# Graph network kernel: the later edge passes take 36 instead of 40 node tiles as products with counts

## The chip, the cores and the metric

The kernel runs on one core of one Trainium2 chip. The metric is the device time of one execution in microseconds (us); lower is better. The engines are named as in the profile: PE multiplies matrices, PEld loads its weights, DVE and ACT work on vectors, POOL issues the indirect DMAs (gathers and scatters by row indices), and SP issues most of the plain DMAs.

## The reference, cut to what matters

A graph of 12500 nodes with 128 features and 200000 edges passes through four layers, each followed by a residual and a layer norm. Each layer adds up, for every node, rows of the nodes at the other end of its edges. Three of the four sums are plain (no weight on the edge once the rows are scaled):

```
msgs = feats[edge_src] * norm[:, None]
agg  = segment_sum(msgs, edge_dst, num_segments=n)        # layer 1, then a top-2 mixture of 64 experts
h    = segment_sum(xs[s], d, num_segments=N)              # layer 2
agg  = segment_sum(x[src], dst, num_segments=x.shape[0])  # layer 3
```

The edges are sorted by `dst`, and `dst` is drawn as `12500 * u ** 2` with `u` uniform. So low node numbers have many edges and high ones few: about half of the edges end in the first quarter of the nodes. `src` is uniform.

## The kernel before, in words

Nodes are handled in 98 tiles of 128, edges in 391 steps of 512 (four chunks of 128). Rows of features are kept in HBM tables as three bfloat16 parts whose sum is the float32 value, so a matrix product with a table tile is three products.

The stages follow one another:

1. `spread_edges` and `collect_edges` (up to about 2860 us of the profile) do the weighted first layer and bring, for every tile of source nodes, its edges' destinations into `hs` and `hd`.
2. The first plain pass, `edge_sums(AT, tables[0], later=0)` (about 2866 to 3915 us).
3. Routing (to about 4240 us), the 64 experts (about 4246 to 4825 us) and the combining of their outputs (about 4830 to 5120 us), then the batch norm (to about 5300 us).
4. The second plain pass, `edge_sums(AT, tables[1])`, about 5304 to 6042 us, and its node work.
5. The third plain pass, `edge_sums(AT, tables[2])`, about 6220 to 6955 us, and its node work to the end.

A plain pass (`fast_sums`, L1059) adds up the edges in two ways at once. Destinations below `HT[later] * 128` are taken as **products with counts**: for each tile of source nodes there is a matrix of counts (128 sources x destinations, how many edges lead from one to the other), and `dense += x^T counts` (L1089), in banks of 512 destinations, three products per bank. Destinations above are **gathered**: from edge step `LS[later]` on, every chunk of 128 edges has its source rows fetched by an indirect DMA on POOL (`fg<-table,e_row`, L1098), and multiplied by a 128 x 96 matrix of 0 and 1 made by DVE (`fh`, L1104) into a window of 512 destinations (`fps`, L1115). A window is `WC = 16` chunks, that is four steps; it begins with a product with zeros (L1166), and DVE adds it to the sums `AT` at its end (L1175). Edges that a gathered step has below the limit are masked in `e_loc`.

Band 0 is node tiles 0 to 24 (six banks). Its counts are built in the first pass (`Counter`) and written to HBM (`counts[0]`). Band 1 is node tiles 24 to 40 (four banks). Its counts are built while the experts run (48 of the 98 source tiles, L1367) and while their outputs are combined (the other 50, L1398), by `band_counts` (L1183): DVE makes the marks `fs` (L1037) and `fd` (L1039, as wide as the window of destinations that a twelfth of the tile's edges can reach), PE multiplies them (`fb_ps`, L1053), ACT casts each bank (L1055), SP writes the tile's counts to HBM (L1057). The second and third pass load both bands' counts (`fc_a<-counts`) and the source tile (`fc_x<-table`), three buffers each.

Inside a pass the order on PE, DVE, ACT and POOL is the program's (`manual_schedule`, L1148). The work of the products is a list of steps (one bank of one source tile each); it is dealt out evenly over the windows but the last:

```
per = -(-total // (nw - 1))
...
mine = min(per, left)
...
upto = WC * (m + 1) // max(1, mine)
```

In a window, after each step of products, PE does as many chunks as are due. POOL's list holds only the gathers, issued a window ahead, into twelve buffers of four chunks (`fgat`), which is three windows. With `HT = (24, 40)` and `LS = (191, 247)` a later pass has 98 x 10 + 2 = 982 steps and (391 - 247) / 4 = 36 windows, so 29 steps to a window.

In the expert and combining stages the order on each engine comes from a scheduler. An expert is seven transposes (L1348) whose result DVE copies (L1349, L1350), products with the first weights (L1355), the activation on ACT (L1357), fourteen products with the second weights (L1362), and an addition on DVE (L1365). In combining, each of 98 tiles takes two gathers on POOL (`yk<-ybuf,come`, L1402, twelve buffers), which DVE adds (L1405).

Of the kernel before, what the change touches and what calls it, by code (L numbers as in the profile page):

```python
# [55 lines left out]
MID = NB // 2  # L56
SG = 2 * GM
W3 = 3 * W0 + 6
HT = (24, 40)

HB = 12
LS = (191, 247)
LB = EB // P * LS[0]
NLB = NBLK - LB
LW = 96
# [53 lines left out]

BANDS = Band(0, HT[0]), Band(HT[0], HT[1])  # L120
WM = max(max(b.cols) for b in BANDS)
# [4 lines left out]
def gnn_kernel(ctx: ExitStack, tc: tile.TileContext, a, out: bass.AP):  # L126
# [43 lines left out]
    e_loc = [const.tile([P, NLB], BF16, name=f"e_loc{i}") for i in range(2)]  # L170
    l_slot = const.tile([1, NB - LS[0]], I32, name="l_slot")
    l_base = const.tile([1, (NB - LS[0]) // 4], I32, name="l_base")
    iota_h = const.tile([P, WM], FP16, name="iota_h")
# [159 lines left out]
    def window_slots(pool, first, bad):  # L333

        n = NB - LS[0]
        f = pool.tile([1, n // 4, 4], F32, name="ws_f")
        V.tensor_copy(f.rearrange("o w q -> o (w q)"), first[:, LS[0]:NB])
        V.tensor_copy(l_base, f[:, :, 0])
        for i in range(2):
            V.tensor_scalar(bad[0:1, 10 + i:11 + i], f[:, (LS[i] - LS[0]) // 4, 0:1], float(HT[i] * P), None, op0=OP.is_ge)  # L340
        d = pool.tile([1, n // 4, 4], F32, name="ws_d")
# [111 lines left out]
    def spread_edges(bad):  # L453
# [5 lines left out]
        with tc.tile_pool(name="sc", bufs=1) as pc, tc.tile_pool(name="scp", bufs=1, space=PSUM) as pps:  # L459
# [30 lines left out]
            if True:  # L490
# [3 lines left out]
                with tc.tile_pool(name="rf", bufs=1) as pa, tc.tile_pool(name="rfp", bufs=2, space=PSUM) as tp_:  # L494
# [56 lines left out]
                    for i in range(2):  # L551

                        m = pa.tile([P, NLB], F32, name="in_band")
                        V.tensor_scalar(m, to_c, float(HT[i] * P), -1.0e3, op0=OP.is_lt, op1=OP.mult)
                        V.tensor_tensor(e_loc[i], place, m, OP.add)
# [503 lines left out]
    def fast_sums(AT, table, later):  # L1059
# [7 lines left out]
        with ExitStack() as st:  # L1067
# [5 lines left out]
            V.memset(zeros_b, 0.0)  # L1073
            V.memset(AT[:, HT[later] * P - BANK:], 0.0)
            if build:
# [443 lines left out]
```

## Time and profile before

| | |
|---|---|
| median of 10 runs | 7157.5 us (7154.34 to 7164.61) |
| profiled execution | 7158.06 us, span 7156.3 us |
| PE busy | 5137.7 us (72%) |
| DVE busy | 4252.7 us (59%) |
| POOL busy | 3861.0 us (54%) |
| ACT busy | 2000.4 us (28%) |
| gathers L1098 | 1952, 988 ns each |
| products L1089 | 7424 recorded, 381 ns each |
| moved by DMA | 1375.92 MB, 192 GB/s over the span |

The durations of products are from start to modelled end and overlap; what a product costs in a row of products is read from the distance of their starts. The busy shares are of the whole span, over stages with different limits. Gathers of the three passes share one line: 800 of the 1952 are in the first pass, 576 in each later one.

### The profile page before, as it was taken

What the parts mean: (1) busy time and instruction counts of PE and PEld (TensorE: products, weight loads), DVE (VectorE), ACT (ScalarE), POOL (GpSimd) and SP (SyncE); (2) the same over time, 40 slices, a digit from 0 to 9 for tenths busy, and PEclk for the clock granted to TensorE, in tenths of its full rate; (3) what the DMA queues carried; (4) which work ended last, traced back from release to release, by engine and by line L of the source; (5) the groups of instructions that cost most, each with busy time, mean ns of one, the idle gap of its engine ahead of it and who ended that gap; (6) DMA issues with size and microseconds to landing.
All of it is one profiled execution on the core that took longest, in us unless ns stands there. A gap on an engine that the chain in (4) does not pass through costs nothing. (4 is left out here: it accounts for less than half of the span.)

```text
span 7156.3 us, 106164 instructions
## 1 busy us (share of the span) xinstructions
PE 5137.7 (72%) x32622; PEld 3146.0 (44%) x33009; DVE 4252.7 (59%) x11539; ACT 2000.4 (28%) x4124; POOL 3861.0 (54%) x3917
## 2 busy tenths in 40 slices
PE   0666666666665664899996659998539998299995
PEld 0444444444442332455553437663215554155544
DVE  6887777777785777767673854549861112611115
ACT  3333333333331222333331114444420000300003
POOL 0677777777771000777777550007427775177760
PEclk7555555555557887999997669999769998599998
DMA  9976545555558997455553125554358886588862
GB/s 249 268 222 202 156 152 152 152 151 152 152 148 271 322 321 229 153 166 167 165 164 119 39 90 166 165 159 134 127 176 294 287 282 216 165 292 290 282 227 67
DMA packets 1045604, 1375.92 MB, mean 192 GB/s; under 512 B 106204, under 2 KB 848216, under 8 KB 1045038
## 3 DMA queue, kind: packets, MB, share of 16 engines
q1 hardware_dynamic: 802680, 960.66, 43.9%
q0 software_dynamic: 181312, 376.38, 16.8%
q10 hardware_dynamic: 61046, 31.77, 1.6%
q8 instruction: 301, 4.93, 0.3%
q14 instruction: 265, 2.17, 0.1%
HBM read 911.40 MB, written 457.00 MB: 191 GB/s over the span
## 5 line engine op out<-in xcount | busy, mean ns | idle before, releaser
L1098 POOL DMA_INDIRECT fg<-table,e_row x1952 | 1928.5, 988 | 1658.5 <-SPq L987 681.4
L1089 PE MATMUL dense<-fc_a,fc_x 128*128 128x512 bf16 x7424 | 1870.1, 381 | 253.1 <-DMA fc_x<-table 185.8
L715 POOL DMA_INDIRECT msg<-rows,to x1564 | 1509.3, 965 | 656.9 <-issue 381.1
L1089 PEld LDWEIGHTS <-fc_x 128*128 128x128 bf16 x7644 | 678.4, 98 | 830.9 <-issue 249.9
L1175 DVE TENSOR_TENSOR AT<-AT,fps 128x512 f32 x122 | 84.0, 688 | 1606.8 <-PE fps L1115 1583.7
L1053 PE MATMUL fb_ps<-fd,fs 128*128 128x512 bf16 (+7 forms) x3942 | 879.2, 341 | 88.5 <-DMA fg<-table,e_row 44.3
L665 PE MATMUL g_ps<-rows,minus 128*128 128x258 bf16 x1564 | 462.8, 400 | 617.7 <-ACT rows L698 583.4
L698 ACT CAST rows<-g_ps 128x516 bf16<-128x516 f32 x1173 | 698.7, 596 | 647.1 <-PE g_ps L665 294.8
L659 PE MATMUL g_ps<-win,hot 128*128 128x129 bf16 x4692 | 651.0, 311 | 238.5 <-DMA win<-table 120.1
L1039 DVE TENSOR_SCALAR fd<-iota_h,hd 128x128 bf16<-128x128 f16 (+6 forms) x1563 | 786.7, 509 | 0.0
L1115 PEld LDWEIGHTS <-fg 128*128 128x128 bf16 x5856 | 463.4, 98 | 517.5 <-DMA fg<-table,e_row 86.1
L659 PEld LDWEIGHTS <-hot 128*128 128x128 bf16 x4692 | 534.4, 143 | 318.9 <-issue 199.5
L1115 PE MATMUL fps<-fh,fg 128*128 128x96 bf16 x5856 | 579.4, 209 | 86.9 <-DMA fg<-table,e_row 68.7
L831 PE MATMUL ce_sum<-ce_r,ce_s 128*128 128x390 bf16 x1764 | 380.9, 383 | 274.9 <-DVE ce_s L828 269.0
L1402 POOL DMA_INDIRECT yk<-ybuf,come x196 | 219.8, 1121 | 652.6 <-DMA counts<-bc_a 593.1
L1053 PEld LDWEIGHTS <-fs 128*128 128x128 bf16 x4108 | 377.7, 98 | 387.6 <-issue 124.4
L665 PEld LDWEIGHTS <-minus 128*128 128x128 bf16 x1564 | 199.8, 128 | 744.3 <-issue 743.9
L1055 ACT CAST fc_a<-fb_ps 128x512 bf16<-128x512 f32 x588 | 344.1, 585 | 633.0 <-PE fb_ps L1053 615.4
L643 DVE TENSOR_TENSOR_SCAN run_ps<-one_ps,run_ps,bin 99x512 f32<-99x512 f32 x390 | 505.4, 1296 | 13.8
L1037 DVE TENSOR_SCALAR fs<-iota_b,hs 128x128 bf16<-128x128 bf16 x1563 | 409.5, 264 | 38.3 <-PE fb_ps L1053 34.7
L831 PEld LDWEIGHTS <-ce_s 128*128 128x128 bf16 x1764 | 190.3, 112 | 465.5 <-DVE ce_s L828 261.3
L232 ACT ACTIVATE ln_sq<-zz,ln_m 128x128 f32<-128x128 f32 x392 | 152.0, 389 | 813.2 <-DVE ln_m L228 813.2
(378 smaller groups left out, 6299.6 us busy)
## 6 DMA issues: line engine op xcount, KB each, us to landing
ce_r<-msg SPq DMA_DIRECT2D x98, 1782.0 KB
fc_a<-counts SPq DMA_DIRECT2D x196, 768.0 KB
fc_a<-counts SPq DMA_DIRECT2D x196, 512.0 KB
rb<-rows_d SPq DMA_DIRECT2D x391, 256.0 KB
counts<-fc_a SPq DMA_DIRECT2D x98, 768.0 KB
counts<-bc_a SPq DMA_DIRECT2D x98, 512.0 KB
fc_x<-table SPq DMA_DIRECT2D x490, 96.0 KB
msg<-blank SPq DMA_DIRECT2D x99, 396.0 KB
```

Of the source, the lines that this page charges most:

```text
L643: V.tensor_tensor_scan(c, one_ps, b, st["end"], OP.mult, OP.add)
L659: T.matmul(gps[i][:, q, 0:D + 1], hot[i][:, q * P:(q + 1) * P], win[i][:, k, :], start=(q == 2 * half and k == 0), stop=False)
L665: T.matmul(gps[i][:, 2 * h:2 * h + 2, 0:D + 1], minus, r[:, 2 * h:2 * h + 2, k * W0:k * W0 + D + 1], start=False, stop=True, skip_group_ch ...
L698: S.copy(r[:, :, k * W0:k * W0 + D + 1], gt)
L715: sc = G.indirect_dma_start(out=msg[:, :], out_offset=bass.IndirectOffsetOnAxis(ap=to[:, q:q + 1], axis=0), in_=r[:, q, :], in_offset=None)
L831: T.matmul(ps, sel[:, j, :], r[:, j, 0:3 * W0], start=(j == 0), stop=(j == RB - 1))
L1037: V.tensor_scalar(sel, iota_b, hs[:, s, j:j + 1], None, op0=OP.is_equal)
L1039: V.tensor_scalar(col[:, 0:hi - lo], iota_h[:, 0:hi - lo], hd[self.i][:, s, q:q + 1], None, op0=OP.is_equal)
L1053: T.matmul(ps[:, lo - c0:hi - c0], self.sel[s, j], self.col[s, j][:, lo - w[j][0]:hi - w[j][0]], start=(j == first), stop=(j == js[-1]))
L1089: T.matmul(dense[n], xr[s][:, k, :], cnt[s][:, n * BANK:(n + 1) * BANK], start=(s == 0 and k == 0), stop=(s == NT - 1 and k == 2))
L1098: G.indirect_dma_start(out=g[q][:, i].rearrange("p k f -> p (k f)"), out_offset=None, in_=table[:, :], in_offset=bass.IndirectOffsetOnAxis ...
L1115: T.matmul(ps[:, ds(at[0], LW)], g[i // 4][:, i % 4, k, :], hot[i // 4][:, i % 4, :], start=False, stop=(i == WC - 1 and k == 2))
```

## The change

Two constants change; no function does.

```diff
-HT = (24, 40)
+HT = (24, 36)
 
 HB = 12
-LS = (191, 247)
+LS = (191, 235)
```

Band 1 becomes node tiles 24 to 36, three banks instead of four. The later passes have 98 x 9 + 2 = 884 steps of products, and gather the edges from step 235 on, twelve steps more: (391 - 235) / 4 = 39 windows, 624 gathers a pass, and 24 steps to a window. `band_counts` makes three banks per source tile: of an ordinary tile the 17 products with marks become 13 (the four of the last bank, 512 columns each, fall away), and the six marks `fd` that were 2048, 2048, 1472, 1216, 640 and 320 wide become 1536, 1536, 1216, 960, 320 and 128 wide. A tile's counts in HBM shrink from 512 to 384 KB. The first pass keeps its band 0 and its step 191.

## The prediction

> **What bounds the kernel now.** I began with the page: its busy rows show where the engines are full. The page's slices (tenths of busy time, each 178.9 us):
>
> ```profile
> PE   0666666666665664899996659998539998299995
> POOL 0677777777771000777777550007427775177760
> PEclk7555555555557887999997669999769998599998
> ```
>
> Four stretches have PE at 9: the first edge pass (slices 17 to 20, counted from 0), the experts (24 to 26) and the two later edge passes (30 to 32 and 35 to 38). POOL stands at 7 in all three passes. "9" and "7" suggest that PE is the bound and POOL has a quarter to spare. So I asked for busy time, granted clock and DMA in stretches inside these stages; the columns are length, then PE, PEld, DVE, ACT, POOL busy us (instructions), clock, DMA share, GB/s.
>
> ```profile
> 3850.00:3910.00 60.00, 24.09 (x147) 14.79 (x147) 7.68 (x15) 0.00 (x0) 45.52 (x48) 0.50 0.28 78
> 4250.00:4820.00 570.00, 566.10 (x3395) 399.41 (x3456) 291.42 (x703) 245.06 (x430) 0.00 (x0) 1.00 0.56 164
> 4850.00:5100.00 250.00, 209.61 (x822) 83.88 (x838) 230.69 (x726) 114.65 (x199) 196.95 (x175) 0.99 0.41 139
> 5400.00:6000.00 600.00, 594.49 (x3791) 302.82 (x3866) 76.48 (x149) 0.00 (x0) 455.25 (x476) 1.00 0.86 286
> 6300.00:6900.00 600.00, 595.74 (x3798) 303.11 (x3873) 74.39 (x144) 0.00 (x0) 455.33 (x476) 1.00 0.86 287
> ```
>
> Row 1 is the end of the first pass, where the products are done and only gathers are left: PE idles, the DMA engines are at 0.28, and POOL still shows 76% busy. Thus 76% is a POOL that is full. POOL's waits in the second pass say why (who waited for whom: total us, times, longest):
>
> ```profile
> POOL fg L1098 <- issue: 137.1, 439, 3.6
> POOL fg L1098 <- PE dense L1089: 19.5, 64, 0.3
> POOL fg L1098 <- PE fps L1115: 11.9, 39, 0.3
> ```
>
> Every gather has the same 0.30 us of idle time before it, whoever is named; once 3.6, at the start. POOL never waits for a buffer that PE must free. POOL's timeline gives its pace; one row each early and late in the second pass, then in the third (start, us):
>
> ```profile
> 5319.90 0.94 POOL L1098 DMA_INDIRECT fg<-table,e_row  x1 [3.62 <-issue]
> ...
> 6037.21 0.95 POOL L1098 DMA_INDIRECT fg<-table,e_row  x1 [0.30 <-issue]
> 6227.41 0.95 POOL L1098 DMA_INDIRECT fg<-table,e_row  x1 [0.30 <-issue]
> ...
> 6950.51 0.94 POOL L1098 DMA_INDIRECT fg<-table,e_row  x1 [0.30 <-issue]
> ```
>
> The first is gather 8 of 576 and the second the last: 717.3 us / 568 = 1.263 us. The third is gather 4: 723.1 / 572 = 1.264 us. In the stretch of row 1 it is 1.26 us as well, so neither DMA load nor PE makes this pace. A window of 16 gathers costs POOL 20.2 us. PE needs 21.0 us for it now (zeroing products at 5990.52 and 6011.56 us); it falls behind by up to two windows, which the three windows of buffers hold, and catches up in the last two windows, which have no products. Both engines thus end the pass within a microsecond or so of each other: PE is full, and POOL is full too.
>
> **The change, part by part.** *Later passes.* Removed per pass: 98 source tiles x 1 bank x 3 = 294 products of 512 columns. Six take 1.30 us in PE's rows, so one takes 0.2165 us: -63.7 us of PE work. Added: three windows (39 for 36), 144 products of 96 columns at 0.043 us (three in 0.13 us between products) and three zeroings at 0.22: +6.8 us on PE. Added on POOL: 48 gathers x 1.263 = +60.6 us, and none removed. The steps of a window fall from 29 to 24 (884 of them over 38), so PE needs 24 x 0.65 + 16 x 0.13 + 0.22 = 17.9 us against POOL's 20.2. The products' saving becomes waiting, and the pass follows POOL: +60.6 us, twice, is +121.3. The order of instructions shows that POOL's list grows by exactly 48 in each pass. What follows the last gather stays: its landing (6950.51 to 6954.19 us in the third pass), three small products and one addition.
>
> At nothing: the wider clearing of AT on DVE (512 more of 8448 columns in 7.1 us, 0.4 us) and 12 more comparisons and three more additions for the gathers run on a DVE that is 13% busy; uncovered they would cost 0.4 + 12 x 0.55 + 3 x 0.69 = 9 us a pass. The loads fall from 512 to 384 KB per source tile and pass, in a queue that is at 0.86 and will have more time.
>
> *Experts.* 48 source tiles of counts are built here, now with 13 instead of 17 products on PE, which is 99% busy. The four that go have 512 columns: 192 x 0.2165 = -41.6 us by their own length. The rows offer a second reading. Their lines below are the last group of products of experts four apart, early and late (start, us):
>
> ```profile
> 4285.63 3.27 PE L1362 MATMUL pw<-w,hT 128*112 128x128 f32 x28
> 4318.56 3.27 PE L1362 MATMUL pw<-w,hT 128*112 128x128 f32 x28
> ...
> 4441.21 3.28 PE L1362 MATMUL pw<-w,hT 128*112 128x128 f32 x28
> 4478.24 3.27 PE L1362 MATMUL pw<-w,hT 128*112 128x128 f32 x28
> ```
>
> Early, four experts take 32.93 us with 34 count products between them (two tiles); late, 37.03 with 51 (three). A tile is 7744 columns, 3.27 us at 0.2165 per 512, yet the third costs 4.10: late in the stage the marks of L1037 and L1039 stand on DVE ahead of the copies of L1349 that the next expert waits for. In the order of the changed kernel nearly all experts have the early form (26 count products to three experts, the copies right behind L1365). Early form: (32.93 - 2 x 3.27) / 4 = 6.60 us per expert without counts. New stage: 64 x 6.60 + 558 products (42.9 tiles of 5696 columns, 2.41 us) = 526, against 578 now (4246.3 to 4824.5): -52 us. I take -48, nearer to the second, since it is read from rows of the very pattern; range -40 to -54. Lost cover: the early form keeps 6 or 7 count products between L1348 and L1355, 1.2 us for a copy of about 1.0.
>
> *Combining.* 50 tiles are counted while POOL gathers yk back to back (4830.06 to 5108.28 us, 1.427 us each; the last bracket shows again only 0.3 us waits):
>
> ```profile
> L1402 POOL DMA_INDIRECT yk<-ybuf,come x196 | 219.8, 1121 | 652.6 <-DMA counts<-bc_a 593.1 <-DVE fs L1037 20.1 <-DMA yk<-ybuf,come 17.1
> ```
>
> Here a gather lasts 1121 ns, against 946 for the median fg: 34 us over, while DVE is 92% busy. The marks shrink: widths 2048, 2048, 1472, 1216, 640, 320 took 745, 745, 593, 541, 376, 308 ns; at 1536, 1536, 1216, 960, 320, 128 I interpolate 610, 610, 541, 465, 308, 250, so 0.53 us less per tile, 26 us in all. If POOL's pace ignored that, the gain were 0; if DVE set the stage, 26. The rows say POOL sets it and is stretched beside DVE; the marks, 75 us of L1037 and 164 of L1039, lose 26 of 240: by share 34 x 26 / 240 = 4 us, more if long marks delay more. I take -6, and -2 for the eight products that the last two tiles lose behind the last gather. [...]
>
> **Sum:** +121.3 - 48 - 8 = +65. The profiled execution took 7158.06 us (span 7156.3), 0.6 above the median of the ten: 7158 + 65 = 7223 us.
>
> **Rivals.** *A: PE is the bound, so the kernel gets faster.* For it: PE at 99%, and the chain of waits puts 82% of the second pass on the products. Then each pass changes by -63.7 + 6.8 = -57, and the sum is -114 - 56 = -170: 6988 us. It would need a gather pace of (727 - 57) / 624 = 1.07 us or less. The whole change breaks even when a pass grows by 28 us, that is at (576 x 1.263 + 28) / 624 = 1.21 us; no start-to-start distance of fg rows in the stretches that I read is under 1.24. Chance 4%.
>
> *B: the clock.* PE will wait in the later passes, and waits cost it clock. In the first pass's end:
>
> ```profile
> 3842.39 0.43 PE L1115 MATMUL fps<-fh,fg 128*128 128x96 bf16 x3 [2.42 <-DMA fg<-table,e_row]
> ...
> 3843.64 1.48 PE L1089 MATMUL dense<-fc_a,fc_x 128*128 128x512 bf16 x3
> ```
>
> After a wait of 2.42 us three products take 1.48 us instead of 0.81, for some 4 us. PE needs 17.9 of 20.2 us, so it becomes the bound where the mean clock falls below 0.89; at 0.75 a window is 23.9 us, 37 of them 884 against 794 for the whole pass, +90 twice: about 7400 us. Against it: the combining stretch is 84% busy with many waits at a clock of 0.99, a chunk's wait here is about 2.3 / 16 = 0.14 us, and a PE that falls behind no longer waits. Chance 6%. [...]
>
> *C: something like nothing.* POOL's pace eased to about 1.21, or gains outside the passes doubled: 7158 us, 2%. That the change doesn't do what it says needs edges below step 235 beyond node 4607, and the branch to the general path; the reference's inputs have node 4522 there, so under 1%.
>
> **How the numbers follow.** My forecast has 88%. Low end: passes +118 (added gathers at 1.23), experts -54, combining -26: +38, 7196. High end: passes +123 (at 1.28), experts -40, combining 0, and up to 9 for half-clock stretches behind waits: +92, 7250. The rivals lie outside, so the range holds about 85%. A measurement of this kernel tells 0.2% (14 us) from no change. Faster has A's 4%, same C's 2%, slower the rest, 94%.
>
> **What would show it.** Right: 624 gathers per pass at 1.26 us from end to end, still only 0.3 us before each; PE in the passes below 90% with waits for fg; passes about 60 us longer; experts about 48 shorter. Wrong: gathers that wait, a pace under 1.21, a clock under 0.89 in the passes, or an expert period that stays at 9 us.

## The result and the profile after

The changed kernel took 7206.76 us (median of 8 runs, 7204.25 to 7210.37), the kernel before 7157.5 us on the same chip (28 runs, 7148.0 to 7164.61). The ratio is 1.007, 95% interval 1.0061 to 1.0079: 49 us slower. The forecast was 65 us slower, 7223. The profiled execution of the changed kernel took 7201.54 us, span 7199.8. Four later runs, those with halved marks, were timed while the kernel before itself took 8278 to 8426 us, so of their times only the ratio to it is read.

The page's slices of the changed kernel, each now 180 us:

```profile
PE   0666666666665653999996659987089994499975
POOL 0677777777771000777776640037077773477760
PEclk7555555555557887999997679999599996799988
```

PE still stands at 8 and 9 in the two later passes (slices 29 to 32 and 35 to 37), POOL at 7. By this view alone little has happened. The stretches show more. The first row lies in the experts, the second in the combining, the third and fourth in the later passes; the columns are length, then PE, PEld, DVE, ACT, POOL busy us (instructions), granted clock, DMA share, GB/s.

```profile
4250.00:4770.00 520.00, 514.57 (x3193) 381.48 (x3253) 262.33 (x682) 208.50 (x379) 0.00 (x0) 1.00 0.56 166
4790.00:5040.00 250.00, 187.86 (x701) 76.28 (x712) 224.68 (x785) 95.69 (x166) 192.15 (x190) 0.95 0.38 126
5250.00:5900.00 650.00, 604.73 (x3810) 306.66 (x3885) 84.25 (x163) 0.00 (x0) 493.41 (x515) 1.00 0.82 261
6250.00:6900.00 650.00, 601.10 (x3799) 305.38 (x3874) 84.05 (x163) 0.00 (x0) 493.74 (x514) 1.00 0.81 261
```

In the passes PE went from 99% to 604.73 / 650 = 93% at a clock of 1.00, and POOL is at 493.41 / 650 = 76%, the share of a POOL that is full. Who waits for whom in the second pass of the changed kernel (total us, times, longest): first POOL's longest groups of waits, then PE's.

```profile
POOL fg L1098 <- issue: 157.3, 505, 3.6
POOL fg L1098 <- PE dense L1089: 19.5, 64, 0.3
POOL fg L1098 <- DMA fg<-table,e_row: 8.5, 28, 0.3
```

```profile
PE fps L1115 <- DMA fg<-table,e_row: 63.4, 75, 3.7
PE fps L1115 <- issue: 5.7, 18, 0.5
```

POOL still never waits for a buffer: 0.3 us before every gather, and once 3.6 at the start, as before. PE now waits for gathers that have not landed, 63.4 us in one pass, where the kernel before has 3.0 us. POOL's timeline gives the pace: gather 9 of the second pass and its last one, number 623, counted from 0.

```profile
5247.38 0.94 POOL L1098 DMA_INDIRECT fg<-table,e_row  x1 [0.30 <-issue]
...
6022.99 0.95 POOL L1098 DMA_INDIRECT fg<-table,e_row  x1 [0.30 <-issue]
```

775.6 us / 614 = 1.263 us, as before. The stages side by side, in us, each from the first or last start of the instructions named:

| stage | before | after | difference | forecast |
|---|---|---|---|---|
| to the experts (first L1348) | 4246.3 | 4244.5 | -1.8 | 0 |
| experts (first L1348 to last L1362) | 578.1 | 531.6 | -46.5 | -48 |
| to the first yk | 5.7 | 5.9 | +0.2 | 0 |
| combining: first to last yk | 278.2 | 256.8 | -21.4 | -6 |
| last yk to the second pass's first gather | 195.4 | 189.8 | -5.6 | -2 |
| second pass, first to last gather | 733.5 | 794.4 | +60.9 | +60.6 |
| to the third pass | 183.2 | 182.2 | -1.0 | 0 |
| third pass, first to last gather | 730.1 | 792.6 | +62.5 | +60.6 |
| to the end | 205.8 | 202.1 | -3.7 | 0 |

The differences add to +43.6, the two spans differ by 43.5. Two of the three big terms, the passes and the experts, hold to about 2 us. The third, combining, is three times what I forecast:

```profile
L1402 POOL DMA_INDIRECT yk<-ybuf,come x196 | 198.3, 1012 | 605.7 <-DMA counts<-bc_a 546.3
```

A gather of yk takes 1012 ns on average where it took 1121, and 196 x 0.109 = 21.4 us is the whole of that stage's gain.

### The profile page after: what moved, and what is told of

It is laid out like the page before. It is cut to its first block, busy times and chain, and to the rows that moved or that the text cites. A ratio compares the mean times of both kernels' runs of the same rounds, so it can differ in the third digit from the quotient of the medians.

```text
span 7199.8 us, 105218 instructions
## 1 busy us (share of the span) xinstructions
PE 5012.6 (70%) x31949; PEld 3093.2 (43%) x32324; DVE 4215.2 (59%) x11567; ACT 1936.2 (27%) x4026; POOL 3931.7 (55%) x4013
## 5 line engine op out<-in xcount | busy, mean ns | idle before, releaser
L1098 POOL DMA_INDIRECT fg<-table,e_row x2048 | 2023.7, 988 | 1677.3 <-SPq L987 678.0
L1089 PE MATMUL dense<-fc_a,fc_x 128*128 128x512 bf16 x6842 | 1770.0, 381 | 254.4 <-DMA fc_x<-table 244.9
L1089 PEld LDWEIGHTS <-fc_x 128*128 128x128 bf16 x7056 | 611.8, 98 | 751.6 <-DMA fc_x<-table 194.6
L1053 PE MATMUL fb_ps<-fd,fs 128*128 128x512 bf16 (+6 forms) x3557 | 775.5, 338 | 92.8 <-DMA fg<-table,e_row 44.3
L1115 PE MATMUL fps<-fh,fg 128*128 128x96 bf16 x6144 | 659.7, 208 | 233.1 <-DMA fg<-table,e_row 190.6
L1115 PEld LDWEIGHTS <-fg 128*128 128x128 bf16 x6144 | 500.3, 98 | 734.5 <-DMA fg<-table,e_row 286.6
L1039 DVE TENSOR_SCALAR fd<-iota_h,hd 128x128 bf16<-128x128 f16 (+5 forms) x1563 | 733.9, 475 | 0.0
L1402 POOL DMA_INDIRECT yk<-ybuf,come x196 | 198.3, 1012 | 605.7 <-DMA counts<-bc_a 546.3
L1053 PEld LDWEIGHTS <-fs 128*128 128x128 bf16 x3717 | 342.7, 98 | 357.7 <-issue 114.7
```

The source lines that it names most:

```text
L1039: V.tensor_scalar(col[:, 0:hi - lo], iota_h[:, 0:hi - lo], hd[self.i][:, s, q:q + 1], None, op0=OP.is_equal)
L1053: T.matmul(ps[:, lo - c0:hi - c0], self.sel[s, j], self.col[s, j][:, lo - w[j][0]:hi - w[j][0]], start=(j == first), stop=(j == js[-1]))
L1089: T.matmul(dense[n], xr[s][:, k, :], cnt[s][:, n * BANK:(n + 1) * BANK], start=(s == 0 and k == 0), stop=(s == NT - 1 and k == 2))
L1098: G.indirect_dma_start(out=g[q][:, i].rearrange("p k f -> p (k f)"), out_offset=None, in_=table[:, :], in_offset=bass.IndirectOffsetOnAxis ...
L1115: T.matmul(ps[:, ds(at[0], LW)], g[i // 4][:, i % 4, k, :], hot[i // 4][:, i % 4, :], start=False, stop=(i == WC - 1 and k == 2))
```

## The experiments

My theory: POOL's pace of 1.26 us per gather sets the later passes; PE's saving there is worth nothing; the gains lie in the experts, where PE is full, and in the combining, where the marks on DVE lengthen POOL's gathers. The rival of the first part is that PE is the bound of the passes (A). The rivals of the last part are that the fourth bank's products, casts and writes made the difference, or the busy DVE as such.

**The gathers alone.** Against the kernel before: forty tiles stay as products with counts, twelve more steps are gathered.

```diff
-LS = (191, 247)
+LS = (191, 235)
...
-            V.memset(AT[:, HT[later] * P - BANK:], 0.0)
+            V.memset(AT[:, HT[later] * P - (1 + later) * BANK:], 0.0)
```

> Half of the change alone: the later passes gather from step 235 on (39 windows, 624 gathers) but keep the products of 40 node tiles, and band 1 keeps four banks of counts; edges below node 5120 are masked in the added windows, so the sums stay whole. AT is cleared from 512 columns earlier. Theory (POOL's pace of 1.26 us sets the later passes): 48 gathers x 1.263 = +61 us per pass, first to last gather 794 us as in the changed kernel; PE needs 26 x 0.65 + 2.3 = 19.2 us of the 20.2 us window and still waits; experts and combining as before; 7157 + 122 = 7279 us (7270 to 7290). Rival (PE sets them): only +6.8 us per pass for the small products, 7171 us, and POOL with idle times over 0.3 us.

Measured: 7287.17 us, ratio 1.0175 (1.0158 to 1.0192), 125 us slower. The passes' gathers take 798.6 and 794.2 us, at 1.27 us each; experts (578.8) and combining (280.4) are as before.

**The products alone.** The kernel before, in whose later passes the last bank of band 1 is left out. No gather is added.

```diff
+        use = (BANDS[0].banks, BANDS[1].banks - 1)
...
-                        for n in range(BANDS[b].banks):
+                        for n in range(use[b]):
```

> The other half alone: the kernel before, whose later passes leave out the products of the last bank of band 1 (294 products a pass) and add no gather; counts are built and loaded in full. The sums of node tiles 36 to 40 are left out. Theory (POOL's pace): 576 gathers still take 727 us, so each pass changes by -3 to +1 us, although PE loses 64 us of work; PE busy in the passes falls to about 92%; 7150 to 7158 us. Rival (PE sets them): -64 us per pass, 7030 us.

Measured: 7167.92 us, ratio 1.0009 (0.9999 to 1.0018). That is 10 us above the top of the range expected, and no run isolates why. Taking 64 us of work from PE in each pass bought nothing: 736.4 and 733.6 us from first to last gather, some 3 us more than before. The stretch of the second pass, first of the gathers-only kernel, then of this one:

```profile
5350.00:5950.00 600.00, 577.71 (x3663) 294.01 (x3736) 77.53 (x151) 0.00 (x0) 456.09 (x473) 1.00 0.83 272
```

```profile
5350.00:5950.00 600.00, 563.39 (x3635) 284.01 (x3707) 76.33 (x148) 0.00 (x0) 455.79 (x474) 1.00 0.89 292
```

PE's share differs from kernel to kernel, POOL's is 456 of 600 in both and 455 before; the passes follow the number of gathers and not PE's work. Rival A is dead: it had 7171 for the gathers alone and 7030 here.

**The changed kernel without its added gathers**: 36 windows.

```diff
-        nw = (NB - LS[later]) // (WC // 4)
+        nw = (NB - LS[later]) // (WC // 4) - 3 * later
```

> The changed kernel without its added gathers: the later passes take three windows fewer than they need (36 windows from step 235 on); the edges of the last twelve steps are left out. It holds the experts, the combining and the fewer products of the change. Theory: the passes are as long as before (734 us first to last gather), experts -47 and combining -27 us as in the changed kernel, 7157 - 77 = 7080 us (7072 to 7088), which is 125 us below the changed kernel for 96 gathers, 1.26 to 1.30 us each. Rival (PE sets the passes): a further -64 us per pass, 6955 us.

Measured: 7093.39 us, ratio 0.9909 (0.9892 to 0.9925): 68 us below the kernel before on the same chip (7161.59), and 5 us above the range expected; the profiled execution, 7085.78, lies inside it. The passes' gathers take 736.9 and 733.0 us, as with the products alone; the experts take 531.5 us, yk's stretch 260.3. This is what experts and combining give by themselves, and the changed kernel spends it, and 49 us more, on its added gathers.

**Old widths of the marks.** The changed kernel, but in the combining stage each mark `fd` is made as wide as before; the added columns are not used.

```diff
+                wide = self.i == 1 and s >= EXB
+                mk = {1536: 2048, 1216: 1472, 960: 1216, 320: 640, 128: 320}.get(hi - lo, hi - lo) if wide else hi - lo
...
-                V.tensor_scalar(col[:, 0:hi - lo], iota_h[:, 0:hi - lo], hd[self.i][:, s, q:q + 1], None,
+                V.tensor_scalar(col[:, 0:mk], iota_h[:, 0:mk], hd[self.i][:, s, q:q + 1], None,
```

> The changed kernel, with the marks fd of the combining stage drawn as wide as before (2048, 2048, 1472, 1216, 640, 320; the columns beyond the three banks are not used). Products, casts and writes stay as in the changed kernel. Theory (POOL's gathers yk are stretched beside DVE's marks, and narrower marks are why combining lost 27 us where 8 were forecast): the yk gathers return from 1012 to about 1110 ns, combining to within 5 us of before, 7207 + 22 = 7229 us (7222 to 7234). Rival (the stretch came from the products, casts or writes of the fourth bank): yk stays near 1012 ns, 7207 us. Proportional rule (delay by the share of marks' time): 4 us, 7211 us.

Measured: 7232.15 us, ratio 1.0098 (1.0081 to 1.0115), where the changed kernel has 1.007. The yk row of the run without added gathers, then of this one, both from one chip:

```profile
L1402 POOL DMA_INDIRECT yk<-ybuf,come x196 | 202.0, 1030 | 605.9 <-DMA counts<-bc_a 546.5
```

```profile
L1404 POOL DMA_INDIRECT yk<-ybuf,come x196 | 214.8, 1096 | 606.4 <-DMA counts<-bc_a 546.9
```

The width alone puts back 66 ns a gather, to 1096 ns where about 1110 was expected; yk's stretch is 272.8 us. Over the profiles with four banks, all their marks and 50 tiles in the combining (278.2, 280.4 and 276.5) the mean is 278.4; over those with three and narrow marks (256.8, 260.3 and 257.1, the last from the run that comes next) it is 258.1. So 14.7 of the 20.3 us are the widths (12.5 by the two runs of one chip); for the other 5.6 no run here isolates a cause.

**The fourth bank without its marks.** The changed kernel, in whose combining stage each tile repeats one bank's products and cast and writes 128 KB more.

```diff
+        if s >= EXB:
+            u = cp.tile([P, BANK], BF16, name="bc_u")
+            maker.bank(s, 2, u, again=True)
+            Y.dma_start(spare[s], u)
```

> The changed kernel; in the combining stage each tile repeats one bank's products and its cast, and writes 128 KB more to a spare tensor: the fourth bank's work on PE, ACT and DMA without the wider marks. Theory (marks alone make the difference): yk at 1012 to 1040 ns, its stretch 257 to 263 us, the kernel 7205 to 7214. Rival (the bank's products, cast and write matter): yk back at about 1100 ns, stretch 272 to 278 us, the kernel 7221 to 7229.

Measured: 7216.46 us, ratio 1.0081 (1.0066 to 1.0097), 2.5 us above the theory's range and 4.5 below the rival's; yk 1013 ns, its stretch 257.1 us. The bank's products, casts and writes leave the gathers as they were (1012 ns without them). They lengthen what follows the last gather by 2.3 us (192.1 against 189.8).

**No marks.** The kernel before; tiles up to 96 of the combining stage reuse the marks of two earlier tiles, so their counts are not their own, while products, casts and writes stay in the program.

```diff
-        maker.marks(s, 0, 1)
+        if EXB + 2 <= s < NT - 1:
+            for j in BANDS[1].used(s):
+                for d in (maker.sel, maker.col):
+                    d[s, j] = d[EXB + s % 2, j]
+            dummy(s)
+        else:
+            maker.marks(s, 0, 1)
```

> The kernel before, with 36 windows and four banks of counts. Left out: in the combining stage no marks are made for the tiles up to 96; the products, casts and writes of their counts stay and use the marks of two earlier tiles, so these counts are wrong. Theory (marks on DVE lengthen POOL's gathers): yk falls from 1121 ns to about 950 ns, the pace to about 1.25 us, the stretch of yk from 278 to about 245 us, the kernel by 34 to 40 us, to about 7121. Rival (products, casts or count writes lengthen the gathers, or POOL's pace is what it is): yk stays at 1100 to 1120 ns, the kernel within 7 us of before, about 7157.

Here `dummy` does nothing. Measured: 7234.04 us, ratio 1.0107 (1.0091 to 1.0122), which neither theory expected. The stage itself did as the theory says, yk 961 ns and a stretch of 246.8 us:

```profile
L1411 POOL DMA_INDIRECT yk<-ybuf,come x196 | 188.3, 961 | 652.1 <-DMA counts<-bc_a 592.7
```

But from the last yk to the second pass it is 298.9 us instead of 195.4. ACT's timeline (start, us) has the reason:

```profile
4964.03 0.58 ACT L1055 CAST bc_a<-fb_ps 128x512 bf16<-128x512 f32 x1 [0.55 <-PE fb_ps L1053]
5076.91 1.28 ACT L210 ACT_TABLE_LOAD   x1 [112.29 <-DVE d L1435]
```

Without the marks the scheduler's order differs: an operation of the batch norm stands on ACT's list ahead of the remaining casts. It waits 112 us for DVE, which is adding up yk; the casts queue behind it, PE's products behind the casts, and 103 us of counting are left over after the last gather. The total of this run says nothing of the marks; its gathers do. But from 4964 us on they ran beside hardly any products, casts or writes, so the gathers before that count: the first 14, still beside marks, average 1124 ns, the 94 that start between 4846 and 4964 us, beside products, casts and writes and without marks, 951.

**Reductions in the place of marks.** As above, but `dummy` keeps DVE busy.

```diff
+        for w in (570, 570, 430, 370, 220, 150):
+            for n in (100, w):
+                d = dkp[0].tile([P, 1], F32, name="dm")
+                V.tensor_reduce(d, iota_h[:, 0:n], AX.X, OP.add)
```

> As the run without marks, but in their place DVE does twelve reductions a tile of about the same time in all (one input from SBUF, one column out; 570, 570, 430, 370, 220 and 150 elements and six of 100), so that DVE is as busy as before. The counts are wrong in the same way. Theory (it is the form of the marks that holds up POOL's gathers): yk stays near 950 ns, the kernel at 7115 to 7130. Rival (any busy DVE lengthens them): yk near 1110 ns, the kernel at about 7155.

Measured: 7138.42 us, ratio 0.9969 (0.9958 to 0.998), 8 us above the range of the theory; here products, casts and writes go on through the whole stage. The yk row, the stretch of the combining, and DVE's timeline there:

```profile
L1417 POOL DMA_INDIRECT yk<-ybuf,come x196 | 192.2, 981 | 652.8 <-DMA counts<-bc_a 593.4
```

```profile
4845.00:5085.00 240.00, 211.29 (x890) 96.27 (x908) 235.40 (x760) 124.85 (x216) 182.90 (x188) 0.93 0.48 159
```

```profile
4900.04 3.83 DVE L1190 TENSOR_REDUCE dm<-iota_h 128x1 f32<-128x100 f16 x12
4903.79 0.86 DVE L1420 SCALAR_TENSOR_TENSOR ACC<-yk,gates,ACC 128x128 f32<-128x128 f32 x3
```

The twelve reductions of a tile take 3.75 us from start to start; the twelve marks of a tile in the kernel before take 3.78 (4902.72 to 4906.50 us in its timeline). DVE is even busier than before, 235.40 of 240 us, and the gathers are 140 ns shorter; the stretch is 250.7 us. So what lengthened the gathers was not that DVE is busy (981 ns beside reductions, 961 beside neither reductions nor marks, 1121 beside the marks), and DVE was not the bound of the stage. It is these marks that do it.

**Fewer tiles beside the experts.** The kernel before with `EXB = 44` instead of 48.

> The kernel before with 44 instead of 48 tiles counted beside the experts, so 54 instead of 50 in the combining stage. If a tile of counts costs the experts 4.1 us (the late row) they fall by 16, at 3.27 by 13. In the combining stage the tiles' marks stretch at most: stretch of yk in proportion to the excess per tile, 34 x 4 / 50 = +3, up to +10 if the added tiles also wait. Sum -3 to -13: 7145 to 7155. Rival (the combining stage is full and takes a tile at DVE's price of 5.3 us): +21 - 16 = +5, 7163.

Measured: 7153.81 us, ratio 0.9992 (0.9983 to 1.0001), inside the forecast and not told apart from no change. The experts lose 15.9 us (562.2), 4.0 for each tile: the price that the late rows of the prediction showed. The combining takes 9.7 back, and after the last yk 3.8 us fall away. It is the best version with all the work that ran here, and no more than a hint.

**Halved marks.** By my rows of single gathers, long marks delay out of proportion. In the timeline of before, a gather that starts ahead of two marks of 2048 columns reads:

```profile
4908.49 1.47 POOL L1402 DMA_INDIRECT yk<-ybuf,come  x1 [0.30 <-DVE fd L1039]
```

```profile
4909.03 0.74 DVE L1039 TENSOR_SCALAR fd<-iota_h,hd 128x2048 bf16<-128x2048 f16 x1
...
4909.86 0.74 DVE L1039 TENSOR_SCALAR fd<-iota_h,hd 128x2048 bf16<-128x2048 f16 x1
```

Counted over the whole stage, the 84 gathers of before that overlap a mark of 2048 columns by 0.1 us or more average 1.18 us, the 89 of the changed kernel beside one of 1536 average 1.03. 58 of 196 gathers took 1.2 us or more before, 13 of 196 after. So I halved the widest marks, in the kernel before (n >= 2048) and in the changed one (n >= 1536):

```diff
-                V.tensor_scalar(col[:, 0:hi - lo], iota_h[:, 0:hi - lo], hd[self.i][:, s, q:q + 1], None,
-                                op0=OP.is_equal)
+                n = hi - lo
+                m = n // 2 if self.i and s >= EXB and n >= 2048 else n
+                for a in range(0, n, m):
+                    V.tensor_scalar(col[:, a:a + m], iota_h[:, a:a + m], hd[self.i][:, s, q:q + 1], None,
+                                    op0=OP.is_equal)
```

> The kernel before; in the combining stage each mark of 2048 columns is made by two operations of 1024 (two more operations a tile; DVE's time grows by 2 x 0.14 us a tile, 14 us in all; starts of marks in a row are 0.13 us + 0.26 ns a column apart). Theory (the gathers are held up by the length of the single mark, out of proportion to the sum): yk falls from 1121 ns to about 1050, and its stretch from 278 to 262 to 270 us, since DVE then needs about 270; kernel 7145 to 7156. Rival (it is the sum of the marks' time that counts, as my share-by-time estimate had it): the sum grows by 7%, yk stays at 1121 to 1135 ns, the stretch at 278 to 285, kernel 7160 to 7168.

> The changed kernel; in the combining stage each mark of 1536 columns is made by two of 768 (DVE 14 us more in all, 243 of 257). Theory (length of the single mark): yk falls from 1012 to 965 to 990 ns, its stretch from 257 to 249 to 253, kernel 7198 to 7204. Rival (sum of the marks' time): yk 1012 to 1020 ns, stretch 257 to 259, kernel 7207 to 7211.

> The kernel before with the marks of 2048 columns in the combining stage halved, once more, since the last run of it came from a chip whose gathers took 1.51 instead of 1.26 us throughout. On a chip with 1.26 us: theory (length of the single mark) yk near 1050 ns, stretch 262 to 270 us, kernel 7145 to 7156; rival (sum of the marks' time) yk 1121 to 1135 ns, stretch 278 to 285, kernel 7160 to 7168.

> The changed kernel with the marks of 1536 columns in the combining stage halved, once more for the same reason. On a chip with 1.26 us: theory (length of the single mark) yk 965 to 990 ns, stretch 249 to 253 us, kernel 7198 to 7204; rival (sum of the marks' time) yk 1012 to 1020 ns, stretch 257 to 259, kernel 7207 to 7211.

Measured, as ratios to the kernel before (8425.85 us beside the first two, 8278.41 beside the others): kernel before with halved marks 1.0021 (1.0002 to 1.004) and 1.0034 (1.0017 to 1.005), changed kernel with halved marks 1.0105 (1.0077 to 1.0134) and 1.0123 (1.01 to 1.0145). Taken as ratios, the theory had at most 0.9998 and 1.0065, its rival at most 1.0015 and 1.0075; all four runs lie above both. The expectation's remark that gathers took 1.51 us was a mean with waits in it. In the third run, PE's longest groups of waits over the second pass are

```profile
PE dense L1092 <- issue: 61.1, 74, 4.0
PE fps L1118 <- issue: 27.3, 35, 2.6
```

gaps of PE for which the profile names no cause; POOL then waited for its buffers, up to 8.8 us at once, and its starts in between were still 1.25 us apart. In the combining yk took 1202 ns there, and POOL waited up to 9.9 us for DVE's additions. Single rows can still be set beside those of before, since a gather with no mark beside it has a median of 0.94 us and a mark of 1472 columns takes 0.59 in both. In the third run this gather lies beside pairs of halves of about 0.49 us each:

```profile
5657.79 1.61 POOL L1405 DMA_INDIRECT yk<-ybuf,come  x1 [0.30 <-DVE fs L1037]
```

```profile
5657.40 0.88 DVE L1042 TENSOR_SCALAR fd<-iota_h,hd 128x1024 bf16<-128x1024 f16 x2
...
5658.35 0.88 DVE L1042 TENSOR_SCALAR fd<-iota_h,hd 128x1024 bf16<-128x1024 f16 x2
```

Counted as above, gathers beside halves of 1024 columns average 1.29 us in both runs of them, beside halves of 768 1.22 and 1.17: more than beside the whole marks. Halving did not pay, and these rows speak against the length of the single mark; with POOL's waits mixed in, what does set the delay stays open.

## Why the prediction was right, and where it was off

**The later passes: right, in size and reason.** Forecast +121.3, measured +60.9 and +62.5. The step that decided was to take 76% busy as a full POOL, because a stretch in which little else ran (PE 24.09 of 60 us) showed the same 76%, and because POOL's waits were all 0.3 us. The two halves of the edit, run apart, gave +125 (with all of it in the gathers) and nothing. PE's waiting came as forecast but smaller in the busy column: I had PE under 90%, it is at 93%. My 17.9 of 20.2 us counted distances of starts; the busy column counts each triple of small products to its modelled end (0.29 us and more, where its start-to-start distance is 0.13), so it overstates a PE that is interrupted often: the 32 windows that begin in 5250 to 5900 us need 32 x 17.9 = 573 of 650 us, 88%. The clock was 1.00 in both stretches, with half speed (0.50 for 3.4 us behind the longest) behind single waits only, and rival B did not appear.

**The experts: right.** Forecast -48, measured -46.5, and -46.6 without the added gathers. The late rows now show the early form. PE's timeline of the changed kernel has, three experts apart,

```profile
4449.64 3.27 PE L1362 MATMUL pw<-w,hT 128*112 128x128 f32 x28
...
4474.46 3.27 PE L1362 MATMUL pw<-w,hT 128*112 128x128 f32 x28
```

24.82 us or 8.3 per expert, where before late experts took 37.03 / 4 = 9.3 and the early form would give 8.2. The fewer tiles beside the experts, 4.0 us each, show from the other side that a tile there cost more than its products.

**The combining: the term that was mis-sized.** Forecast -8, measured -27 in the two profiles. The failed step is "by share 34 x 26 / 240 = 4 us, more if long marks delay more. I take -6". The object was right: old widths bring the gathers from 1030 back to 1096 ns, the bank's other work leaves them at 1013, marks replaced by reductions take them to 981. The law was wrong. The time by which a yk exceeds 946 ns fell from 175 to 66 ns, to 0.38 of what it was (84 ns and 0.48 in the run without added gathers), while the marks' time in the trace fell only to 0.91 (217 of 240 us).

The mean yk takes 1121 ns beside the marks, 951 in the 94 gathers counted without them, and 981 beside reductions that take as long in all (3.75 us a tile, the marks 3.78). By what means a mark lengthens a gather, no run here shows. On the size, a delay by the share of the marks' time would have left 0.89 of the excess at the 214 us that I forecast and 0.91 at the 217 measured; 0.38 is far steeper. A delay by that part of a mark which exceeds about 0.5 us would fit. Marks of 2048, 1472 and 1216 columns took 745, 593 and 541 ns before, those of 1536 and 1216 took 610 and 533 ns after: (2 x 0.245 + 0.093 + 0.041) before and (2 x 0.11 + 0.03) after, 0.25 / 0.62 = 0.40. That is an estimate from these lengths, fitted after the fact, and the gather of 1.61 us beside halves of 0.49 us speaks against it. What lengthens the gathers is shown; the law by which it does is not.

**Behind the last yk** the forecast was -2 for the products of the last tiles. The profile pair shows -5.6, but the same stretch is 195.4, 193.5 and 192.8 in three runs with four banks, and 189.8, 190.3 and 190.5 with three: -3.7, of which the repeated bank gives back about 2.

**The rest.** -6.3 us lies in stages that the change does not touch on the path, and their starts differ by more from run to run (the experts began between 4241.6 and 4254.9 us). 1.8 of it stands before the experts, where both kernels do the same. The changed kernel's profiled run was 5.2 us under its median, so the medians differ by 49 and the spans by 43.5.

## What to carry to other kernels

Find the engine that is full by its pace, not by its share (here POOL at 76%, 1.26 us a gather): look for a stretch in which it works alone, and see whether the same pace holds where others are busy. Here two engines ended a pass within a microsecond or so of each other and both were full, and relieving PE of 64 us by loading POOL with 48 gathers cost the whole of the added load: +60.9 and +62.5 us, where 48 x 1.263 is 60.6. Where a queue's instructions last longer than alone, list what runs beside each long one and how long that is, before taking a share of the excess: here a tenth off the neighbour's time (240 to 217 us) took about three fifths off the excess (175 to 66 ns a gather).

## What the runs showed of the hardware that was not expected

- A gather of 128 rows on POOL shows 0.95 us busy and 0.30 idle, 1.26 us on average from start to start, in each of three unlike stretches: before, 3850 to 3910 us, beside a PE at 40% (24.09 of 60 us) and a DMA share of 0.28; before, 5400 to 6000 us, beside a PE at 99% and 0.86; after, 5350 to 5400 us, beside a PE at 94% (46.86 of 50 us) and 0.91. Beside marks of 2048 columns on DVE a single gather took 1.47 us, and the 84 that overlap one averaged 1.18.
- Reductions that keep DVE at 98% (235.40 of 240 us) leave the mean gather at 981 ns, 20 ns above that of the run with no marks and no reductions.
- Single waits of PE were followed by half speed, and not only the one of 2.42 us that the prediction shows. In the second pass after the change the longest, 3.7 us, has six products in 2.76 us behind it where six took 1.46 at full speed, and the granted clock was 0.50 for 3.4 us. A wait of 1.8 us that ended at 5521.05 us had such a stretch 1.1 us behind it too, another of 1.8 us, ended at 5712.97, had none, and over 5250 to 5900 us the mean clock was 1.00. What decides for the shorter waits no run here tests.

```profile
5249.03 0.47 PE L1115 MATMUL fps<-fh,fg 128*128 128x96 bf16 x3 [3.72 <-DMA fg<-table,e_row]
5249.30 2.76 PE L1089 MATMUL dense<-fc_a,fc_x 128*128 128x512 bf16 x6
```

- One operation of the batch norm, placed too early on ACT, cost 103 us in the run without marks (it waited 112 us for DVE, and ACT's casts behind it waited too).
